# Graph attention on Trainium2: the attention output as 32 equal matmuls a batch in place of 24 of two shapes

## The chip, the cores and the metric

The kernel runs on one core of a Trainium2 chip. A core has five engines that work side by side: TensorE (PE in the profile, with its weight loads shown as PEld), VectorE (DVE), ScalarE (ACT), GpSimd (POOL) and SyncE (SP), which issues most of the transfers. The metric is the device time of one execution in microseconds (us), as the median of several runs.

A matmul on PE has a stationary operand (the weights, loaded first) and a moving one, which streams through column by column. [...] 

## What is computed

Sixteen batches of 512 nodes with 512 features. Each node attends to the first 20 nodes of its batch, over 16 heads of 32 features, once along the given adjacency and once along its transpose (two directions, `d`). The reference, cut to the part that matters here:

```python
def _gat_attention(self_feat, cond_adj, label_bias, Wq, bq, Wk, bk, Wout, bout):
    kv = self_feat[:, :ng]                      # ng = 20, dh = 32
    ...
    w = jax.nn.softmax(aff, axis=-1)            # [B, N, 16 heads, 20 keys]
    out_t = jnp.einsum('bnhm,bmf->bnhf', w, kv)
    out = jnp.einsum('bnhf,hgf->bnhg', out_t, Wout) + bout.reshape(H, F // H)
    return out.reshape(B, N, F)

output = self_feat
for d in range(2):
    ...
    output = output + _gat_attention(self_feat, cond, vb, Wq[d], ...)
return exp_v + jax.nn.relu(output)
```

The kernel multiplies the keys' features with `Wout` first, so that the output of a head is one matmul of the softmax weights with a small matrix: for each head, 40 rows (20 keys of two directions) by 32 outputs. Everything is float32.

## The kernel before

Batches run one after another (`b`), each in four tiles of 128 nodes (`nt`). For each tile, PE computes the scores of all heads (`scores`, L366, 64 matmuls of 128 rows and 32 outputs over 152 columns), the tile then passes through VectorE, ScalarE and GpSimd for the mask and the softmax (`weigh`, L380 to L399; `normal`, L416 to L418), and VectorE turns it by 32 x 32 blocks (`turn`, L425) into `wts[b]`. Between the scores PE makes the feature products of the next batch (`product`, L284).

The change touches `attend` (L427 to L440) alone. It is called once for a batch with all 512 nodes of it: while batch `b` is at its tile 2, `attend(b - 1, banks)` (L940) is issued for the batch before it, into the four accumulators `ps_o` (one bank of PSUM for each group of four heads). `finish` (L442) then adds the features on VectorE (L445) and applies the Relu on ScalarE (L447). On PE the call stands between the scores of tile 1 and those of tile 2 of batch `b`. So it is in 15 batches. The last batch has two calls at the very end of the program (L1044), with 384 and with 128 nodes; ahead of each, four matmuls with an identity (`put_self`, L813) put the features into the banks, and behind them VectorE takes a maximum (L1049) and the results are sent. The order of the instructions on each engine is the order in which the code issues them.

In `attend`, `wt` holds the softmax weights with (key, node) laid out so that partition block `a` of 32 belongs to head group `a` (four heads), and the 4 x 40 = 160 keys of the group lie in five blocks `j` of 32. Heads 0 and 1 share block 1, and heads 2 and 3 share block 3. `vd` holds the keys' values for each group as eight columns of 32 outputs, numbered `at` = 2 x head + part: part 0 for the first block that the head touches, part 1 for the second, with zeros in the rows that belong to another head. The moving operand is `wt[r, :, ts(j, 32)]`: 32 rows by 512 columns (16 groups of 32 nodes).

Before, the first four columns of the table `runs` give: two pairs, one on block 1 (heads 0 and 1 at once) and one on block 3 (heads 2 and 3), with 64 outputs, each for four groups: 8 matmuls of 32 x 64, which start the sums. Then 16 single ones of 32 x 32 for blocks 0, 2, 2 and 4, which complete them. In every call that is 24 matmuls. Each matmul of float32 stands in the trace as two weight loads and two matmul records.

## Time and profile before

| | |
|---|---|
| median of 3 runs | 581.49 us (580.59 to 582.52) |
| span of the profiled execution | 578.9 us |
| matmul records of `attend` (L436) | 816 |
| busy time of those records | 36.9 us of PE's 572.2 us |
| granted TensorE clock | 0.998 |

The profile was taken of one execution; the span is the time from its first instruction to its last. Busy time counts the time in which an engine had at least one instruction running; matmuls overlap, so the mean duration of one record is longer than its share. In a group's row, "L436 PE MATMUL ps_o<-wt,vd 32*64 32x512 f32 x240 | 17.3, 612" reads: line 436, matmul, result `ps_o` from `wt` and `vd`, weights of 32 rows and 64 outputs, 512 columns of 32 rows moving, 240 records, 17.3 us busy, 612 ns for one. In a row of the chain, the first number is the start and the second the length of a stretch of work, both in us, and the count is that of its records.

### The profile page before, as it was taken

The numbers are of one execution on the slowest core, as the hardware profiler recorded it, in microseconds if no ns is written. First come the engines' busy times: TensorE is split into PE (matmuls) and PEld (weight loads), VectorE is DVE, ScalarE is ACT, GpSimd is POOL, SyncE is SP. The second block draws the span as 40 slices with busy tenths as digits, with TensorE's granted clock in tenths as the row PEclk, the third lists the DMA queues.
The fourth block names the chain that finished last, engine by engine and source line by source line (L and its number), as shares of the span: only waits on it lengthen the run. The fifth ranks groups of instructions, "written<-read, shape, count | busy, mean of one in ns | idle before, by whom it ended". The sixth has DMA issues, their size and how long they took to land.

```text
span 578.9 us, 31006 instructions
## 1 busy us (share of the span) xinstructions
PE 572.2 (99%) x13508; PEld 434.1 (75%) x13508; DVE 492.9 (85%) x790; ACT 393.6 (68%) x1162; POOL 404.6 (70%) x383
## 2 busy tenths in 40 slices
PE   9999999999999999999999999999999999999996
PEld 6544458888878787878778787877887878787873
DVE  0675776979898989898999999898989898989896
ACT  1234554687878777778786868687887877777571
POOL 2726986658586776858585867776858677785874
PEclk9999999999999999999999999999999999999999
DMA  8998997867777767777676777566666766674404
GB/s 315 382 396 283 333 361 233 237 195 219 209 233 185 220 187 204 213 185 228 167 220 166 222 166 220 164 206 180 204 193 192 195 192 189 192 208 111 147 19 147
DMA packets 98788, 123.26 MB, mean 213 GB/s; under 512 B 18877, under 2 KB 66969, under 8 KB 96605
## 3 DMA queue, kind: packets, MB, share of 16 engines
q1 hardware_dynamic: 96268, 117.54, 67.8%
q0 software_dynamic: 1392, 2.43, 1.8%
q8 instruction: 106, 1.74, 1.3%
q10 hardware_dynamic: 992, 1.31, 0.6%
q14 instruction: 30, 0.24, 0.1%
HBM read 82.30 MB, written 40.24 MB: 212 GB/s over the span
## 4 chain that ended last, share of the span: by engine, by line
PE 98%; DVE 1%; issue 0%; DVEq 0%
PE ps_s L366 46%; PE ps_a L284 19%; PE ps_c L284 9%; PE ps_o L436 6%; PE ps_d L284 5%; PE ps_v L658 3%; PE ps_k L598 3%; PE ps_kv L541 1%; PE ps_o L813 1%; PE ps_warm L500 1%; PE ps_nz L214 0%; PE ps_s L355 0%; PE _g(2, 2, 0, 14, 16)0_845 L692 0%; PE _g(0, 2, 0, 14, 16)0_448 L692 0%; PE g(3, 2, 0, 14, 16)0_1055 L692 0%
## 5 line engine op out<-in xcount | busy, mean ns | idle before, releaser
L366 PEld LDWEIGHTS ps_s<-g,sf 128*32 128x32 f32 x8192 | 263.6, 110 | 21.9 <-issue 14.8
L366 PE MATMUL ps_s<-g,sf 128*32 128x152 f32 x8192 | 278.1, 293 | 0.7 <-issue 0.7
L338 ACT COPY both<-add 32x80 f32<-32x80 f32 x512 | 130.9, 256 | 60.9 <-DVE add L329 55.1
L418 POOL TENSOR_TENSOR s<-s,sm 128x640 f32<-128x640 f32 x63 | 80.4, 1275 | 96.8 <-DVE sm L417 52.5
L345 POOL TENSOR_TENSOR full<-cq,both 128x640 f32<-128x640 f32 x64 | 100.3, 1568 | 26.9 <-issue 20.9
L318 ACT ACTIVATE prod<-adj,wb_sb 128x80 f32<-128x80 int32 x330 | 112.4, 432 | 0.0
L393 ACT ACTIVATE s<-s 128x640 f32<-128x640 f32 x63 | 46.5, 738 | 56.0 <-DVE s L388 55.6
L450 POOL TENSOR_TENSOR o<-o,x 128x512 f32<-128x512 f32 x60 | 76.3, 1293 | 0.0
L380 DVE TENSOR_TENSOR full<-ps_s,full 128x608 f32<-128x608 f32 x63 | 48.6, 772 | 22.5 <-PE ps_s L366 19.4
L284 PE MATMUL ps_a<-t,ws_s 128*32 128x246 f32 x1024 | 59.8, 371 | 0.0
L416 DVE TENSOR_REDUCE sm<-s 128x32 f32<-128x640 f32 x63 | 50.8, 807 | 10.5 <-ACT s L393 10.3
L384 DVE TENSOR_REDUCE ps_s<-full 128x32 f32<-128x640 f32 x63 | 52.2, 828 | 2.2
L425 DVE STREAM_TRANSPOSE wt<-s 128x640 f32<-128x640 f32 x63 | 52.8, 838 | 0.6 <-POOL s L418 0.6
L388 DVE TENSOR_TENSOR s<-full,ps_s 128x640 f32<-128x640 f32 x63 | 51.5, 818 | 1.1
L290 DVE SCALAR_TENSOR_TENSOR sf<-nz,qw,ps_a 128x246 f32<-128x246 f32 x128 | 51.5, 443 | 0.1
L284 PEld LDWEIGHTS ps_a<-t,ws_s 128*32 128x32 f32 x1024 | 34.4, 110 | 16.8 <-issue 0.8
L329 DVE TENSOR_REDUCE add<-prod 128x80 f32<-128x960 f32 x32 | 36.8, 1150 | 7.4 <-ACT prod L318 4.0
L447 ACT ACTIVATE o<-o,bo 128x512 f32<-128x512 f32 x60 | 38.3, 713 | 0.6 <-DVE o L445 0.6
L249 POOL TENSOR_TENSOR t<-x,t 128x492 f32<-128x492 f32 x32 | 36.8, 1151 | 1.3
L436 PE MATMUL ps_o<-wt,vd 32*32 32x512 f32 (+5 forms) x816 | 36.9, 578 | 0.0
L249 POOL TENSOR_TENSOR t<-x 128x492 f32<-128x492 f32 x32 | 36.8, 1151 | 0.0
L445 DVE TENSOR_TENSOR o<-ps_o,sf 128x512 f32<-128x512 f32 x60 | 36.7, 668 | 0.0
(225 smaller groups left out, 715.8 us busy)
## 6 DMA issues: line engine op xcount, KB each, us to landing
g<-g_d SPq DMA_DIRECT2D x60, 304.0 KB
g_d<-st SPq DMA_DIRECT2D x16, 1064.0 KB
out_T<-o SPq DMA_DIRECT2D x60, 256.0 KB
xn<-in_xn SPq DMA_DIRECT2D x56, 256.0 KB
x<-in_xT SPq DMA_DIRECT2D x56, 256.0 KB
adj<-in_adj SPq DMA_DIRECT2D x60, 220.0 KB
nz<-nz_d SPq DMA_DIRECT2D x14, 256.0 KB
wk<-in_wkT SPq DMA_DIRECT2D x2, 1024.0 KB
```

The costliest lines, as they stand in the source:

```text
L249: done["xsum"] = nc.gpsimd.tensor_sub(t, one, two)
L284: nc.tensor.matmul(to, lhs, x[:, k], start=start, stop=stop, skip_group_check=n != 2)
L290: done["partial"] = nc.vector.scalar_tensor_tensor(to[:, i], nzs[b][:, half(l)], qw[:, 2 * f + i, b : b + 1], parts[b, "a"][i][:, :HN], AL ...
L318: nc.scalar.activation(p[:, :, l], a[:, :, l], AF.Identity, scale=wb_sb[:, l : l + 1])
L338: done["spread"] = nc.scalar.copy(adds[b, h][bass.ts(a, R), :, g], add[r].rearrange("p (t m) -> p t m", t=2))
L345: done["full"] = nc.gpsimd.tensor_add(f, cqs[b].unsqueeze(1).to_broadcast(shape), adds[b, nt // 2][:, nt % 2].unsqueeze(2).to_broadcast(sh ...
L366: nc.tensor.matmul(to, sfs[b][:, k, bass.ds(nt * P + (2 * g + j) * R, R)], of, start=(onto is None and k == 0 and (whole or j == 0)), stop ...
L384: nc.vector.tensor_reduce(mx, f, AX.X, ALU.max)
L418: done["normal"] = nc.gpsimd.tensor_mul(s, s, sm.unsqueeze(3).to_broadcast(full))
L425: nc.vector.transpose(wts[b][:, nt], s.rearrange("p a h m -> p (a h m)"))
L436: nc.tensor.matmul(banks[a][bass.ds(at // 2 * DH, n * DH)].rearrange("p (t n) -> p t n", n=32), vd[r, bass.ds(at * DH, n * DH)], wt[r, :, ...
L450: nc.gpsimd.tensor_add(o[:, c], o[:, c], xs[b][:, c])
```

## The change

In place of the table of pairs and singles there are three loops: over the two parts `i`, over the four heads `e` of a group, and over the four groups `a`. All matmuls have 32 rows and 32 outputs. The first sixteen (`i` = 0) start the sums of the sixteen heads, the next sixteen (`i` = 1) complete them. The products are the same; a block with two heads is now passed twice, once for each. In every call that is 32 matmuls.

```diff
-        for first, runs in ((True, ((1, 2, 1), (5, 2, 3))), (False, ((0, 1, 0), (3, 1, 2), (4, 1, 2), (7, 1, 4)))):
-            for at, n, j in runs:
+        for i in range(2):
+            for e in range(HL):
                 for a in range(HL):
                     r = bass.ts(a, R)
                     nc.tensor.matmul(
-                        banks[a][bass.ds(at // 2 * DH, n * DH)].rearrange("p (t n) -> p t n", n=32),
-                        vd[r, bass.ds(at * DH, n * DH)], wt[r, :, bass.ts(j, 32)],
-                        start=start and first, stop=stop and not first,
+                        banks[a][bass.ts(e, DH)].rearrange("p (t n) -> p t n", n=32),
+                        vd[r, bass.ts(2 * e + i, DH)], wt[r, :, bass.ts(e * S // 32 + i, 32)],
+                        start=start and i == 0, stop=stop and i == 1,
                     )
```

The order on PE, first at the call of batch 0 (the other fourteen in the loop are like it). A row names the line, the result's tile, the operands, and the outputs by columns; a count at its end stands for that many of the same. Before, with the eight pairs (each row twice) ahead of the sixteen singles (each row four times):

```order
180 L366 MATMUL ps_s1_1_1819<-g1_1372,sf1_1473 32x152 x64
181 L436 MATMUL ps_o0_0_1929<-wt0_1340,vd0_1781 64x512
182 L436 MATMUL ps_o0_1_1930<-wt0_1340,vd0_1781 64x512
...
188 L436 MATMUL ps_o0_3_1932<-wt0_1340,vd0_1781 64x512
189 L436 MATMUL ps_o0_0_1929<-wt0_1340,vd0_1781 32x512
...
204 L436 MATMUL ps_o0_3_1932<-wt0_1340,vd0_1781 32x512
205 L366 MATMUL ps_s1_2_1916<-g1_1372,sf1_1473 32x152 x64
```

With the change, at the same place:

```order
180 L366 MATMUL ps_s1_1_1819<-g1_1372,sf1_1473 32x152 x64
181 L436 MATMUL ps_o0_0_1929<-wt0_1340,vd0_1781 32x512
182 L436 MATMUL ps_o0_1_1930<-wt0_1340,vd0_1781 32x512
...
196 L436 MATMUL ps_o0_3_1932<-wt0_1340,vd0_1781 32x512
197 L436 MATMUL ps_o0_0_1929<-wt0_1340,vd0_1781 32x512
...
212 L436 MATMUL ps_o0_3_1932<-wt0_1340,vd0_1781 32x512
213 L366 MATMUL ps_s1_2_1916<-g1_1372,sf1_1473 32x152 x64
```

The call has 32 rows in place of 24, of one shape throughout; rows 181 to 196 are the first batch of sixteen, rows 197 to 212 the second. The scores ahead of it and behind it are where they were. In the last batch's calls the same happens between the matmuls with the identity (L813) and the end of the program:

```order
903 L813 MATMUL ps_o_0_2_10661<-biased,ident 128x128 x2
904 L813 MATMUL ps_o_2_2_10662<-biased,ident 128x128
905 L813 MATMUL ps_o_3_2_10663<-biased,ident 128x128
906 L436 MATMUL ps_o_0_2_10661<-wt_10420,vd_10424 32x128 x2
907 L436 MATMUL ps_o_2_2_10662<-wt_10420,vd_10424 32x128
...
929 L436 MATMUL ps_o_3_2_10663<-wt_10420,vd_10424 32x128
930 L1108 UNCONDITIONAL_BRANCH
```

Here rows 906 to 929 are the whole last call, 32 matmuls (a row with x2 stands for groups 0 and 1, whose banks have one name); no other engine's order differs.

## The prediction

> **What bounds the kernel now.** I read the page's busy table and chain of waits first.

> ```profile
> PE 572.2 (99%) x13508; PEld 434.1 (75%) x13508; DVE 492.9 (85%) x790; ACT 393.6 (68%) x1162; POOL 404.6 (70%) x383
> PE 98%; DVE 1%; issue 0%; DVEq 0%
> ```

> TensorE (PE) is busy for 99% of the span of 578.9 us and 98% of the chain that ended last runs over it. What the change adds to or takes from PE's time is the change of the span, unless PE has to wait elsewhere for something. The chain, row by row, gives the places (start, us, engine, tile, line, records):

> ```profile
> 276.94 4.13 PE ps_s L366 x128
> 281.08 2.17 PE ps_o L436 x48
> 283.25 4.27 PE ps_s L366 x128
> 555.38 2.17 PE ps_o L436 x48
> 570.48 1.74 PE ps_o L436 x48
> 573.31 1.01 PE ps_o L436 x45
> ```

> The attention output (`attend`, L436, tile `ps_o`) stands there with 2.17 us in each of 15 batches and twice at the end. Inside one call I took the instructions by shape (mean ns behind the bar) and the timeline of the weight loads (start, us):

> ```profile
> L436 PE MATMUL ps_o<-wt,vd 32*32 32x512 f32 x480 | 17.9, 599 | 0.0
> L436 PE MATMUL ps_o<-wt,vd 32*64 32x512 f32 x240 | 17.3, 612 | 0.0
> L366 PE MATMUL ps_s<-g,sf 128*32 128x152 f32 x8192 | 278.1, 293 | 0.7 <-issue 0.7
> L284 PE MATMUL ps_a<-t,ws_s 128*32 128x246 f32 x1024 | 59.8, 371 | 0.0
> 281.01 0.23 PEld L436 LDWEIGHTS ps_o<-wt,vd 32*64 32x64 f32 x16 [0.24 <-issue]
> 282.05 0.29 PEld L436 LDWEIGHTS ps_o<-wt,vd 32*32 32x32 f32 x32 [0.81 <-issue]
> 283.18 1.06 PEld L366 LDWEIGHTS ps_s<-g,sf 128*32 128x32 f32 x36 [0.84 <-issue]
> ```

> Each matmul is two weight-load and two matmul records (8 pairs are x16 loads, 16 singles x32): two passes. 94 columns more (152 to 246) cost 78 ns, so 0.83 ns a column: 512 columns stream for 0.43 us, and the record's other 0.17 us are its way out. The call takes 283.18 - 281.01 = 2.17 us: 1.04 us of pairs, then 1.13 us of singles, whose loads start only when the pairs are through. Thin windows over `ps_o` count the matmul records that run in each (window, length, PE busy, count):

> ```profile
> 281.00:281.06 0.06, 0.05 (x8) 0.05 (x8) 0.00 (x0) 0.00 (x0) 1.00 0.61 200
> 281.48:281.54 0.06, 0.06 (x16) 0.00 (x0) 0.00 (x0) 0.00 (x0) 1.00 1.03 124
> 282.13:282.14 0.01, 0.01 (x11) 0.01 (x22) 0.00 (x0) 0.00 (x0) 1.00 1.21 474
> 282.15:282.16 0.01, 0.01 (x12) 0.01 (x24) 0.00 (x0) 0.00 (x0) 1.00 0.75 64
> 282.18:282.19 0.01, 0.01 (x14) 0.01 (x23) 0.00 (x0) 0.00 (x0) 1.00 0.18 64
> 282.20:282.20 0.01, 0.01 (x15) 0.01 (x18) 0.00 (x0) 0.00 (x0) 1.00 1.12 410
> 282.21:282.22 0.01, 0.01 (x16) 0.01 (x17) 0.00 (x0) 0.00 (x0) 1.00 0.46 128
> 282.50:282.51 0.01, 0.01 (x17) 0.00 (x0) 0.00 (x0) 0.00 (x0) 1.00 0.58 192
> 282.66:282.67 0.01, 0.01 (x32) 0.00 (x0) 0.00 (x0) 0.00 (x0) 1.00 0.31 65
> ```

> All eight pairs are off within 0.05 us and take their second pass 0.48 us later (x16 in 281.48 to 281.54). Of the sixteen singles, eleven run by 282.14 and the rest drip in to x16 at 282.21, five in 0.08 us: some 0.0165 us each. The second pass follows 0.45 us behind the first (the seventeenth record at 282.50, the thirty-second by 282.66), and the next shape's loads come 0.52 us behind the last second pass: 0.43 of stream, 0.09 until the array is empty.

> **The change part by part.** It takes away 8 pairs and puts 16 singles in their place in each of 17 calls: two batches of sixteen 32-by-32 matmuls of one shape, each batch once over the sixteen places. The loads' waits, the operands and what stands before and behind the call stay. Removed is one change of shape inside the call (0.09 us of emptying, and loads that couldn't run ahead). Added are 8 matmuls, 32 records. Per call in the loop:

> - First batch: starts like the pairs; its first matmul ends its second record at 0.45 + 0.599 = 1.05 us.
> - Second batch: if sixteen are all that is let in, its first starts at 1.05 and its last at 1.05 + 15 x 0.0165 = 1.30 us. That one's second pass starts at 1.75, and the next shape's loads 0.52 later, at 2.27 us. Against 2.17 that is **+0.10 us**.
> - Without a limit: each place runs four passes of 0.45 us on end. Its last place starts 0.10 to 0.16 late (282.05 to 282.21), and 0.10 to 0.16 + 3 x 0.45 + 0.52 = 1.97 to 2.03 us. Against 2.17 that is **-0.14 to -0.20**.
> - Worst bound: all sixteen of the first batch drip (0.25 us instead of 0.16), which delays the second by as much: +0.19.

> I take +0.10, since the limit explains the drip to 0.01 us and nothing else that I found does. [...]

> Fourteen calls of the loop stand between PE work on both sides: 14 x 0.105 = 1.47 us. The fifteenth (555.31) doesn't reach the end, either way up to 0.36 us:

> ```profile
> 561.75 0.81 PE L355 MATMUL ps_s<-full,ident 128*128 128x320 f32 x2
> 562.18 0.73 DVE L380 TENSOR_TENSOR full<-ps_s,full 128x608 f32<-128x608 f32 x1
> 570.41 0.23 PEld L436 LDWEIGHTS ps_o<-wt,vd 32*64 32x64 f32 x16 [0.55 <-DVE mx L399]
> 571.24 0.29 PEld L436 LDWEIGHTS ps_o<-wt,vd 32*32 32x32 f32 x32 [0.60 <-issue]
> 572.15 0.97 PEld L813 LDWEIGHTS ps_o<-biased,ident 128*128 128x128 f32 x8 [0.62 <-issue]
> 574.32 0.27 DVE o L1049
> ```

> The last scores of tile 2 are out at 561.82 (the L355 weight step starts then in the chain), but VectorE (DVE) takes them only at 562.18, behind its own work; and the last batch's first call waits for DVE (mx L399). The two last calls are on PE's path again. The first, with 384 columns (0.32 us of stream, 0.35 from pass to pass), takes 572.15 - 570.41 = 1.74 us. By the window its first matmul is out at 0.35 + 0.32 + 0.17 = 0.84, its thirty-second starts by 1.09, and 0.35 + 0.32 + 0.09 lead to 1.85: +0.11. The second, with 128 columns (0.11 us of stream), comes to about +0.04 in the same way. VectorE's L1049 at 574.32 follows its end. Sum: 1.47 + 0.15 = **+1.6 us**, from a span of 578.9 to 580.5. The median of 581.49 lies 2.6 us above that span (the launch around it, and the spread of the runs); the change doesn't touch these, so **583.1 us**.

> The cover that the gain or loss of the loop needs is VectorE's, the next busiest. One batch (window, length, then the busy us of PE, weight loads, VectorE, ScalarE and GpSimd):

> ```profile
> 250.60:281.08 30.48, 30.48 (x793) 24.21 (x795) 27.84 (x43) 23.48 (x71) 21.95 (x20) 1.00 0.75 204
> ```

> PE is busy for all of the 30.48 us and VectorE for 27.84, so 0.2 us less of PE don't make VectorE the bound. A slower call delays the four additions of `finish` on it by 0.1 us, which nothing on PE waits for until the next batch's call.

> **The rivals.** (1) *No limit; the array stays full over both batches*: -0.19 a call, 14 x 0.19 + 0.1 at the end = -2.8, **578.7 us**. For it: the scores of L366 run 64 matmuls in 4.13 us without gaps at 0.032 us a record, so loads do run ahead where the shape stays. [...] It decides if the second batch's first records start near 0.90 us into the call, at the stream's end of the first. (2) *The limit is freed as a stream ends* (0.88 us), not when the record does (1.05): the second batch's last starts at 0.93 + 0.25 = 1.18 and the call ends at 2.15: -0.02, **581.2 us**. For it: the modelled ends of records aren't exact. Against: the coincidence above would be off by 0.17 us. (3) *No limit, but the second batch waits for the whole first, since it adds to the same sums*: two batches of 1.13 us make 2.26, +0.09, **582.9 us**, about the forecast by another way; the scores, which add 16 matmuls to one sum without a gap, speak against it. (4) *The drip of both batches*, +0.19 a call: 14 x 0.19 + 0.3 = +3.0, **584.5 us**; the ten or eleven that came at once speak against it.

> **How the numbers follow.** The window has 0.46, rival (1) 0.29, (2) 0.08, (3) 0.09, (4) 0.08. A measurement of this kernel tells 0.3% (1.74 us) from no change: 579.75 and 583.23 are the bounds. Rival (1) lies below the lower one, with its milder form (-0.14, 579.4) still under it: faster 0.29. Window and (3) straddle the upper one, since +1.6 us is just short of it and 0.01 us a call moves it by 0.14: of their 0.55 I give 0.37 to slower and 0.18 to no change. With (2) no change has 0.26, with (4) slower has 0.45. The window's own range is 582.4 to 584.0. The range for the time is 578.5 to 584.3; it has to hold rival (1), since that has more than 2 in 10.

> **What would show it.** In the changed kernel's trace the call has x64 records; the windows show sixteen running, then the seventeenth matmul's start. At 1.05 us into the call, and an end at 2.27, the window is right; 0.90 and under 2.05, rival (1). There is one row of loads in place of two, and 0.09 us of emptying remain only at its end. Scores behind the call stay at 4.27 us. If PE's total stays at the old value although the call changed, something else hides it; what would make me wrong beyond that is a second limit that holds the first batch itself.

## The result, and the profile after

The changed kernel takes 583.93 us in the median of 13 runs (581.27 to 585.97), the kernel before 580.68 us in 13 runs beside it (579.28 to 582.52). The ratio is 1.0047, with a 95% interval of 1.0029 to 1.0065: slower, as forecast, but by 3.25 us where the forecast had 1.6; two later comparisons of the same kernel have 1.65 and 1.64 us. The profiled execution has a span of 581.9 us.

The chain of waits of the changed kernel, at the places shown before (start us, us, engine, tile, line, records):

```profile
278.29 4.13 PE ps_s L366 x128
282.42 2.28 PE ps_o L436 x62
284.70 4.27 PE ps_s L366 x128
558.08 2.28 PE ps_o L436 x62
573.29 1.85 PE ps_o L436 x63
576.23 1.02 PE ps_o L436 x56
```

A regular call went from 2.17 to 2.28 us, with the scores on both sides as long as they were (4.13 and 4.27). The batch at the middle of the run, by engine (window, length, then the busy us of PE, weight loads, VectorE, ScalarE and GpSimd):

```profile
282.35:312.94 30.59, 30.59 (x805) 24.52 (x801) 27.83 (x43) 23.48 (x71) 22.05 (x20) 1.00 0.70 191
```

30.59 us in place of 30.48, PE busy for all of it: the loss of a call is the loss of a batch, 0.11 us. The timeline of the weight loads of the same call (start us, us, count, idle time ahead):

```profile
282.35 0.25 PEld L436 LDWEIGHTS ps_o<-wt,vd 32*32 32x32 f32 x32 [0.24 <-issue]
282.81 0.10 PEld L436 LDWEIGHTS ps_o<-wt,vd 32*32 32x32 f32 x1 [0.21 <-issue]
283.24 0.55 PEld L436 LDWEIGHTS ps_o<-wt,vd 32*32 32x32 f32 x31 [0.32 <-issue]
284.63 1.45 PEld L366 LDWEIGHTS ps_s<-g,sf 128*32 128x32 f32 x48 [0.84 <-issue]
```

A place, here and in the recorded texts, is what one pair of a group and a head uses in the kernel: the group's 32 rows and the head's 32 outputs. A call has sixteen of them. The loads of the first sixteen matmuls (x32, two each) are through within 0.25 us. Then one single load comes at 282.81, 0.46 us into the call, where the second passes begin (the matmul records that run go from x16 at 282.79 to x19 at 282.81); the next comes at 283.24, and the rest only after that. Thin windows over the matmul records, and two over the loads, show when the second batch starts (window, length, busy, count; of the first kind the first column after the length is PE, of the second it is the loads):

```profile
283.20:283.22 0.02, 0.02 (x16) 0.00 (x0) 0.00 (x0) 0.00 (x0) 1.00 0.00 0
283.24:283.25 0.01, 0.01 (x17) 0.01 (x1) 0.00 (x0) 0.00 (x0) 1.00 0.00 0
283.41:283.42 0.01, 0.00 (x0) 1.00 1.79 64
283.43:283.44 0.01, 0.01 (x1) 1.00 0.11 1
```

The first place passes on to its second matmul at 283.24 (x17, 0.89 us into the call). All others wait: no load runs at 283.41, and the next one comes at 283.43, 1.08 us into the call. By the forecast's estimate of 0.43 us for a pass that starts at 0.45, the streams of the first batch end from 0.88 us on, so by this estimate the first place goes on within 0.01 us and the other fifteen have nothing to stream for some 0.2 us or more. This gap is what the change costs, and the change of shape that is no longer made (0.09 us by the forecast's estimate, and loads that came only 1.04 us into the call) is what it saves; the balance is the measured 0.11 us.

The span grew by 3.0 us. From the second call of the loop to the fifteenth it went from 555.38 - 159.00 = 396.38 to 558.08 - 160.07 = 398.01 us: +1.63. Of it, 13 x 0.11 = 1.43 are the regular calls and 0.38 the two long ones below; against that, the profile before has one batch of its own that is 0.17 us too long (219.95 to 250.60). The two stretches from the fifteenth call to the last (15.10 to 15.21 us, then 2.83 to 2.94) add 0.22. The second call itself started 1.07 us later, which the later profiles of the same kernel don't repeat (158.83 and 157.98). The first call of the loop varies from 2.28 to 2.81 us in the profiles of the changed kernel and takes 2.68 and 2.70 in those of the one before. Behind it, two calls were longer than the regular ones:

```profile
404.77 2.40 PE ps_o L436 x63
527.23 2.54 PE ps_o L436 x62
```

### The profile page after: what moved, and what is told of

Same layout as the page of the kernel before. It is cut to its first block, busy times and chain, and to the rows that moved or that the text cites. A ratio compares the mean times of both kernels' runs of the same rounds, so it can differ in the third digit from the quotient of the medians.

```text
span 581.9 us, 31550 instructions
## 1 busy us (share of the span) xinstructions
PE 574.4 (99%) x13780; PEld 439.7 (76%) x13780; DVE 493.5 (85%) x790; ACT 393.6 (68%) x1162; POOL 404.5 (70%) x383
## 4 chain that ended last, share of the span: by engine, by line
PE 98%; DMA 1%; DVE 0%; issue 0%; DVEq 0%
PE ps_s L366 46%; PE ps_a L284 18%; PE ps_c L284 9%; PE ps_o L436 6%; PE ps_d L284 5%; PE ps_v L658 3%; PE ps_k L598 3%; PE ps_kv L541 1%; PE ps_o L813 1%; DMA ws_v<-in_wsT 1%; PE ps_nz L214 0%; PE ps_s L355 0%; PE _g(0, 2, 0, 14, 16)0_448 L692 0%; PE g(3, 2, 0, 14, 16)0_1055 L692 0%; PE _g(2, 2, 0, 14, 16)0_845 L692 0%
## 5 line engine op out<-in xcount | busy, mean ns | idle before, releaser
L366 PEld LDWEIGHTS ps_s<-g,sf 128*32 128x32 f32 x8192 | 263.9, 110 | 21.6 <-issue 14.7
L366 PE MATMUL ps_s<-g,sf 128*32 128x152 f32 x8192 | 278.5, 293 | 0.4 <-issue 0.3
L380 DVE TENSOR_TENSOR full<-ps_s,full 128x608 f32<-128x608 f32 x63 | 48.8, 775 | 26.9 <-PE ps_s L366 24.4
L284 PE MATMUL ps_a<-t,ws_s 128*32 128x246 f32 x1024 | 60.3, 371 | 0.6 <-issue 0.6
L284 PEld LDWEIGHTS ps_a<-t,ws_s 128*32 128x32 f32 x1024 | 34.2, 110 | 17.6 <-issue 1.2
L436 PE MATMUL ps_o<-wt,vd 32*32 32x512 f32 (+2 forms) x1088 | 38.8, 574 | 0.4 <-PE ps_s L366 0.4
```

What stands on the lines that cost most here:

```text
L284: nc.tensor.matmul(to, lhs, x[:, k], start=start, stop=stop, skip_group_check=n != 2)
L366: nc.tensor.matmul(to, sfs[b][:, k, bass.ds(nt * P + (2 * g + j) * R, R)], of, start=(onto is None and k == 0 and (whole or j == 0)), stop ...
L436: nc.tensor.matmul(banks[a][bass.ts(e, DH)].rearrange("p (t n) -> p t n", n=32), vd[r, bass.ts(2 * e + i, DH)], wt[r, :, bass.ts(e * S // ...
```

## The experiments

Theory W is that of the forecast, and as there an estimate from the times: at most sixteen matmuls of float32 (64 records, at the four that each has in the trace) are let in ahead, and room is made in order, from the oldest. Theory N has no such limit. The other question was how much of the 3.0 us belongs to the program. All edits but those of `e3_singles_first` and `e6_before_again` are to the changed kernel. The calls' lengths are those of the chain of waits, or the time from a call's first load to the next shape's.

### The two matmuls of a place side by side

```diff
-        for i in range(2):
-            for e in range(HL):
-                for a in range(HL):
+        for e in range(HL):
+            for a in range(HL):
+                for i in range(2):
```

> The same 32 matmuls a call, but the two of one place stand next to each other (loops e, a, i in place of i, e, a). Theory W (at most sixteen matmuls, 64 records, are let in, and room comes only as the oldest is wholly out, in order): the first sixteen matmuls are now those of eight places only, so half of the array stands empty until the second matmul of the first place is out. The first places' second passes and second matmuls run to about 1.95 us into the call, the ninth to sixteenth places start only then, and a call takes 3.9 to 4.0 us in place of 2.28; 15 calls of +1.7 and the two last ones make a span of 607 to 611 us. Theory N (no such limit; the second batch merely waits for the sums of the first): all places are independent, so a call takes 2.0 to 2.3 us and the span is 579 to 582 us. Theory C (a limit of sixteen unfinished matmuls, but freed out of order): the other eight places start at about 0.9 to 1.1 us, a call takes about 3.0 us, and the span is near 594 us.

Measured: 608.4 us in one run (span 606.3). The chain at one call:

```profile
288.94 3.96 PE ps_o L436 x64
```

The timeline of the weight loads of the same call:

```profile
288.86 0.26 PEld L436 LDWEIGHTS ps_o<-wt,vd 32*32 32x32 f32 x17 [0.24 <-issue]
289.32 0.72 PEld L436 LDWEIGHTS ps_o<-wt,vd 32*32 32x32 f32 x18 [0.20 <-issue]
290.37 0.10 PEld L436 LDWEIGHTS ps_o<-wt,vd 32*32 32x32 f32 x1 [0.33 <-issue]
290.80 1.19 PEld L436 LDWEIGHTS ps_o<-wt,vd 32*32 32x32 f32 x28 [0.33 <-issue]
```

The same 32 matmuls take 3.96 us in place of 2.28, for their order alone. By their counts, the first seventeen loads are two for each of eight places and one for the ninth. The first 36 (17, 18 and 1) are then those of the two matmuls in each of these nine; the loads of the other seven places are the last 28, from 290.80 on, 1.94 us into the call. That matmuls merely start in the order of the program does not explain it: by 289.05 eight of them run at once (the window 289.05:289.06 counts x8), although the second matmul of each place stands between them. Theory N (2.0 to 2.3) and the one of a limit freed out of order (3.0) fall; the range that W gave (3.9 to 4.0 us, span 607 to 611) has the call exactly and misses the span by 0.7 us.

### Two halves

```diff
-        for i in range(2):
-            for e in range(HL):
+        for e0 in range(0, HL, 2):
+          for i in range(2):
+            for e in (e0, e0 + 1):
```

> The same 32 matmuls, in the order: first and second part of eight places (heads 0 and 1 of each group), then first and second part of the other eight. Theory W (sixteen matmuls let in, room made in order): the window holds both parts of the first eight places; room comes from 1.05 us on for eight matmuls, which are the first parts of the other places, and their second parts come in only as the first eight's second parts go out, from 1.95 us on. A call takes 2.95 to 3.05 us, against 2.28 with the change and 3.96 with the two matmuls of a place next to each other; span 15 x 0.72 + 0.9 above that of the change, 591.5 to 594 us. Theory N (no limit in order): 2.0 to 2.3 us, 579 to 582 us. A limit freed out of order would let the other eight places start at 0.9 us and give about 2.5 us.

Measured: 591.81 us in one run, span 590.0; with calls of 3.00 us, as W has it. The chain at one call:

```profile
283.85 3.00 PE ps_o L437 x64
```

The span is 1.5 us below the range. That had been 15 x 0.72 + 0.9 = 11.7 us on top of the changed kernel's span, which was 581.9 in the first profile and is 580.8 and 579.5 in the later ones. All three of these hold a long call of batch 13 (below), and here that call takes 3.00 us like the others; the rest of the miss is not accounted for. Between the three orders of the same 32 matmuls there is no other difference than what stands among the first sixteen: sixteen places (2.28 us), eight places twice, with the other half behind (3.00), or two matmuls of a place side by side all through (3.96).

### One batch alone

This kernel leaves out the second part of each head's keys.

```diff
-        for i in range(2):
+        for i in range(1):
...
-                        start=start and i == 0, stop=stop and i == 1,
+                        start=start and i == 0, stop=stop,
```

> Leaves out the second batch of sixteen matmuls in every call (the second part of each head's keys), so a call has 16 matmuls, 8 fewer than before the change. Theory W: the first batch alone takes 1.07 to 1.10 us, so that the second one costs 1.18 to 1.20 us of the 2.28 us where 0.91 (two passes of 0.455) would do if it followed without a gap; the batch period is 30.48 - 2.17 + 1.08 = 29.4 us. If the change costs beyond the calls, by the number of PE instructions (the program's code is longer by 544 records), the span comes out below 578.9 - 15 x 1.09 - 1.3 = 561.3 us by another 1 us or more; if only the calls count, it is 560.5 to 562.5 us.

Measured: 572.01 us, span 570.0. The calls take 1.08 to 1.09 us as expected, so the second batch of the changed kernel costs 1.19. The sum on top of them was wrong (560.5 to 562.5 us were expected for the span): two windows from one call to the next show the length of a batch.

```profile
247.10:277.45 30.35, 29.99 (x774) 25.03 (x770) 27.85 (x44) 24.02 (x74) 22.39 (x20) 1.00 0.77 215
366.98:396.83 29.85, 29.63 (x772) 24.75 (x769) 27.79 (x44) 23.53 (x72) 22.07 (x19) 1.00 0.66 195
```

The waits of PE and of its loads (engine, line, releaser: us in total, times, longest):

```profile
PE ps_a L284 <- DVE sf L290: 3.5, 13, 0.8
PEld ps_a L284 <- POOL s L418: 9.7, 14, 1.2
```

These two batches take 30.35 and 29.85 us, not the 29.4 that 1.08 us less a call would give. PE now waits in its products (L284) for VectorE, and its loads there for GpSimd. With PE at 30.48 us a batch, the others are at best 0.6 us behind it; a gain of up to 0.6 a batch is passed on, and the rest meets them. So the run says nothing on a cost by the number of instructions, for which it was also meant. It fits the prediction's reading that 0.2 us less of PE would have been passed on.

### Singles first

```diff
-        for first, runs in ((True, ((1, 2, 1), (5, 2, 3))), (False, ((0, 1, 0), (3, 1, 2), (4, 1, 2), (7, 1, 4)))):
+        for first, runs in ((True, ((0, 1, 0), (3, 1, 2), (4, 1, 2), (7, 1, 4))), (False, ((1, 2, 1), (5, 2, 3)))):
```

> The kernel before with its two stages swapped: 16 single matmuls first, then 8 pairs. Theory W: the sixteen singles fill the window and all start within 0.10 to 0.12 us; the pairs come in only as the singles go out, from about 1.08 us, and drip at 0.0165 us each; a call takes 2.16 to 2.20 us, as before (2.17), and the time stays within 0.3%. Theory N: the singles start within 0.10 us and the pairs, all issued by then, start within 0.05 us once the array is empty at 1.07 us: a call takes 2.10 us, 0.07 us less, time -1.1 us (-0.2%). In the trace the pairs' first passes tell the two apart: 0.0165 us each (W) or 0.0067 us each (N).

Measured: 580.25 us in 10 runs against 580.55, ratio 0.9986 (0.9969 to 1.0003): no difference that can be told. The loads of a call:

```profile
251.64 0.25 PEld L436 LDWEIGHTS ps_o<-wt,vd 32*32 32x32 f32 x32 [0.24 <-issue]
252.73 0.27 PEld L436 LDWEIGHTS ps_o<-wt,vd 32*64 32x64 f32 x16 [0.84 <-issue]
253.81 0.42 PEld L366 LDWEIGHTS ps_s<-g,sf 128*32 128x32 f32 x16 [0.81 <-issue]
```

253.81 - 251.64 = 2.17 us. The loads alone don't tell the theories apart, as the sixteen loads of the pairs took 0.23 us before, too. The pairs' second passes do, each of which starts 0.48 us behind its first one in the profile before. Thin windows count the matmul records as they join the eight first passes:

```profile
253.20:253.21 0.01, 0.01 (x8) 0.00 (x0) 0.00 (x0) 0.00 (x0) 1.00 0.00 0
253.23:253.24 0.01, 0.01 (x12) 0.00 (x0) 0.00 (x0) 0.00 (x0) 1.00 0.00 0
253.30:253.31 0.01, 0.01 (x16) 0.00 (x0) 0.00 (x0) 0.00 (x0) 1.00 0.00 0
```

Four pairs follow within 0.03 us, the other four over the 0.07 us behind, some 0.0165 each. Before, all eight were off within 0.05. So, as W has it, half of the pairs had been let in by the time the singles were through (N has all eight), and the rest drip in; the call is no shorter than the 2.17 us of before.

### The changed kernel and the one before, again

No edit.

> The changed kernel once more. Its profiled span was 3.0 us above that of before, of which the regular calls (+0.11 us in each of 14 batches) and the end make 1.9 us; +0.6 us came before the first call of attend and two calls were 0.12 and 0.26 us longer than the others. If those are accidents of one execution, this profile has them elsewhere or not at all, every regular call is 2.28 us again, and the ratio to before is 1.0025 to 1.0045. If they belong to the program (its instructions are longer on PE, and fetched in other places), the same two calls are long again, the first call starts at 128.5 us again, and the ratio is 1.0045 to 1.0060.

> The changed kernel a third time. Regular calls 2.28 us. If the call of batch 13 (the fourteenth in the loop) is long by a stall that belongs to its place in the program, it is 2.5 to 2.7 us here too, as in the two profiles so far; if that was an accident, 2.28. Ratio to before 1.0025 to 1.0047.

> The kernel before once more, against itself: ratio 1.000 with an interval that shows what such a comparison can tell (about 0.2% to either side). Its profile shows again 2.17 us a regular call; if single long calls come by accident anywhere, it has one or two of 0.1 to 0.4 us more; if they belong to places in the program, the call of batch 10 (433.4 us) is the only one that is longer, by 0.03 us.

Measured: the changed kernel 582.20 us (12 runs, before 580.55), ratio 1.0025 (1.0008 to 1.0042), and 582.07 us (7 runs, before 580.43), ratio 1.0029 (1.0017 to 1.0041). The kernel before against itself: 0.9990 (0.9979 to 1.0001), so such a comparison has some 0.1% of its own. Regular calls are 2.28 and 2.17 us in all of them; in the second profile of the kernel before, no call behind the first is longer. The chain of the third profile of the changed kernel, around its one long call:

```profile
494.43 2.28 PE ps_o L436 x61
525.02 2.69 PE ps_o L436 x64
556.02 2.28 PE ps_o L436 x62
```

The timeline of the loads of that call:

```profile
524.95 0.23 PEld L436 LDWEIGHTS ps_o<-wt,vd 32*32 32x32 f32 x30 [0.24 <-issue]
525.82 0.56 PEld L436 LDWEIGHTS ps_o<-wt,vd 32*32 32x32 f32 x33 [0.63 <-issue]
526.70 0.10 PEld L436 LDWEIGHTS ps_o<-wt,vd 32*32 32x32 f32 x1 [0.32 <-issue]
```

The call of batch 13 is long in all three profiles of the changed kernel, and each time after fifteen matmuls (x30 loads): the loads pause for 0.48 to 0.65 us before the sixteenth's, and the second batch comes late with them. It costs 0.26, 0.42 and 0.41 us. The other long call of the first profile (404.77) was regular in the two later ones: an accident. So was the late second call.

The two other orders of the 32 matmuls, which have as many records, show the same break at the same place, at no cost. The loads of the two side by side, at the call of batch 12 and at that of batch 13:

```profile
515.35 0.26 PEld L436 LDWEIGHTS ps_o<-wt,vd 32*32 32x32 f32 x17 [0.24 <-issue]
515.80 0.72 PEld L436 LDWEIGHTS ps_o<-wt,vd 32*32 32x32 f32 x18 [0.20 <-issue]
547.61 0.23 PEld L436 LDWEIGHTS ps_o<-wt,vd 32*32 32x32 f32 x16 [0.24 <-issue]
548.07 0.18 PEld L436 LDWEIGHTS ps_o<-wt,vd 32*32 32x32 f32 x7 [0.22 <-issue]
```

At batch 13 the loads at 548.07 stop after seven, those of the second matmuls of seven places: the sixteenth matmul of the call, the second one of the eighth place, is late again. With two halves, the first loads of that call are 16 in place of 17. Both calls keep their length (3.96 and 3.00 us); by W, what was let in before keeps PE busy.

### Everything 64 records later

```diff
-        for i in range(2):
+        for k, i in enumerate((0, 0, 1) if b == 0 else (0, 1)):
...
-                        start=start and i == 0, stop=stop and i == 1,
+                        start=start and i == 0, stop=stop and i == 1 or (b == 0 and k == 0),
```

> The changed kernel with the first sixteen matmuls of the first call issued twice (the second time overwrites the first), so that everything behind them stands 64 PE records later in the program. Theory W: the additional batch costs 1.05 us in that call, and the ratio to before is by 0.0018 above that of the changed kernel. If the long call of batch 13 comes from a place in the program (PE's instructions arriving late there), its stall moves by 64 records, out of the sixteenth matmul of that call and into another part of it or out of it; if it stays at the sixteenth matmul of that call, it comes from what the kernel does there.

Measured: 583.63 us in 4 runs against 580.43, ratio 1.0054 (1.0039 to 1.0069), 0.0025 above the changed kernel beside it where 0.0018 was expected; the intervals are wider than that difference. The timeline has the first loads of the call of batch 13:

```profile
526.88 0.25 PEld L436 LDWEIGHTS ps_o<-wt,vd 32*32 32x32 f32 x32 [0.24 <-issue]
```

The chain, three batches earlier, has a stretch of scores that elsewhere takes 4.13 us:

```profile
430.75 4.43 PE ps_s L366 x128
```

All 32 loads of that call's first batch come at once again; the call is regular. So the stall does not belong to what that call does: with as many records ahead of it, it is there in five profiles of three orders, and with 64 more it is gone in the one profile taken. It goes with the place in PE's program. Whether the 0.30 us more in the scores at 430.75 are the same stall is not shown: 64 records would move it only into the scores right ahead of the call of batch 13, and single delays come by accident elsewhere. What causes it no record here shows; that PE's instructions arrive late there is an assumption of the expectation.

## Why the prediction was right or wrong

**The bound** was right: PE is busy for the whole batch before and after (30.48 and 30.59 us), and the 0.11 us of a call come out as 0.11 us of a batch.

**The limit** (the window of the recorded texts) agrees with the calls' lengths, nearly to their size. The forecast had the second batch starting at 1.05 us, the last of it at 1.30, and the end at 2.27, +0.10 us a call; measured are 1.08 and 2.28, +0.11. The order of the matmuls, which none of the rivals lets matter, changes the call to 3.00 and 3.96 us, each within the range that the limit gave beforehand. The prediction had inferred it from one coincidence of times and given it 0.46; that coincidence used a mean over both passes (0.612 us), where the pairs' second passes take 0.587, and still holds to 0.02 us. No run shows such a limit itself, or its size of sixteen; what they show is 32 loads within 0.25 us, one more at 0.46 us, and the eighteenth matmul's at 1.08. Whether loads and matmuls are counted (64) or matmul records alone (32) they don't tell either, as each matmul here has two of both. The 0.09 us of emptying at a change of shape, which is in the forecast's sums, no run shows either: it was the difference of 0.52 and an estimated 0.43 us. What they show is 0.84 us without a load ahead of the next shape's loads, before and after alike (283.18 and 284.63).

**One sign of it was put wrongly.** The prediction said that the seventeenth matmul's start would be at 1.05 us by the limit and at 0.90 by the first rival. It came at 0.89, and yet the calls have the lengths that the limit gives. The step that failed is "sixteen matmuls (eight pairs and eight singles) are let in ahead, and the next only once the oldest is wholly out": by the loads, room seems to be made record by record. The first load of the seventeenth is in at 0.46 us (the single load at 282.81) and its first matmul record runs at 0.89 (283.24), while the eighteenth's first load comes at 1.08 (283.43), behind the oldest matmul's second pass (the matmul records that run fall from x17 at 283.38 to x16 at 283.40, 1.05 us into the call). The eighteenth is the one that tells.

**The fifteenth call** failed: "doesn't reach the end, either way up to 0.36 us". From that call to the next went from 15.10 to 15.21 us. The 0.36 us were read from VectorE, which takes the last scores of tile 2 late; but what starts the last batch's first call is not VectorE. The chain has PE work (L813) up to that call without a gap, before and after alike:

```profile
567.70 2.78 PE ps_o L813 x8
570.51 2.78 PE ps_o L813 x8
```

The row's "[0.55 <-DVE mx L399]" is idle time of the weight loads, during which the matmuls of L813 ran. The loss is +0.11, not 0.

**The last two calls** came as worked out: the first took 1.85 us, the figure of the prediction. For the second, +0.04 us were forecast; in the chain its length went from 1.01 to 1.02.

**A term was missing**: the stall of 0.26 to 0.42 us at the call of batch 13. The prediction moved 32 records a call through PE at no other cost than their own; that another number of records can also bring a stall into a call was not in it.

With fifteen calls of 0.11 (1.65), 0.11 for the one behind, and about 0.4 for the stall, the trace accounts for 2.2 us, 0.37%, where the forecast had 1.6. The three comparisons give 0.47, 0.25 and 0.29%; the traces' 0.37% lies within the intervals of the three, and so does the forecast's 0.28% of the latter two. The first one's 0.47% has no cause of its own that the profiles repeat. The time, 583.93, lies within the range of 578.5 to 584.3, and that it would be slower had the largest chance. Part of that is luck. By the prediction's own bound of 583.23 for slower, its sum of 583.1 was no change, and so are the two later medians, 582.20 and 582.07. That the first comparison lies above the bound is due to an excess that these did not repeat. What the traces bear out is the term of 0.10 us a call.

**The rivals.** (1) and (2) fall by the call's length, and with the order of the matmuls; the sum of (2) starts from 0.93 us where its own condition gives 0.88, but with either it ends at 2.10 to 2.15 us and not at 2.28. (3), the second batch waiting for the sums of the first, came within 0.02 us of the call's length and needed other witnesses: the first place passes to its second matmul, which adds to the same sums, at 0.89 us, 0.01 us behind the estimated end of its stream, and with the two matmuls of a place side by side it would give 2.0 to 2.3 us, not 3.96. (4), the drip of both batches, would have had 2.36 us.

## What to carry to other kernels

With many small matmuls at once, look at when the loads of each come, and not only at how many matmuls run: here the first sixteen float32 matmuls of a call had their 32 loads within 0.25 us, and of the next sixteen one load came at 0.46 us, the second at 0.89, and the eighteenth matmul's first at 1.08. Try the order, too: here the same 32 matmuls took 2.28 us with the two of one place as far apart as can be, 3.00 with eight places at a time, and 3.96 with the two next to each other, so the order alone was worth 1.7 us. To remove a change of shape is not a gain by itself: the call went from 2.17 to 2.28 us. By W, eight pairs left room for eight of the singles behind them, and sixteen singles leave none for the next batch.

## What the runs showed of the hardware that was not expected

The first load of the seventeenth matmul came in 0.62 us ahead of that of the eighteenth (282.81 and 283.43), which speaks for room that is counted in records. The order of the matmuls changes the call: a limit freed out of order would, by the expectations, have given calls of about 3.0 and 2.5 us where 3.96 and 3.00 were measured. And at one place in PE's program the loads pause for 0.48, 0.65 and 0.63 us in the three profiles of the changed kernel, after the same matmul (x30 loads); in two other orders with as many records the break is at the same place and costs nothing, and with 64 records more ahead of it that call has none.
